# Gate projections of two tiles as one block of seven quarter products, in a one-core Mamba-2 layer

## The chip, the cores and the metric

The kernel runs on one core of a Trainium2 chip. The metric is the device time of one execution in microseconds (us); lower is better. The engines of the core work side by side, each in the order of its own queue: TensorE (PE, matmuls; PEld is its weight load), VectorE (DVE), ScalarE (ACT), GpSimd (POOL) and SyncE (SP), which here issues most of the DMAs.

## What is computed

Two blocks follow each other on x of shape (2, 512, 512), all in fp32. The first is an autocorrelation block with a small mixture of experts. The second, which the change is about, is a Mamba-2 mixer times a gated feed-forward. Cut to that part (B = 2 batches, S = 512 positions, model width 512, inner width 8192 = 128 heads of 64, 8 groups of 16 heads, state 128, chunks of 128):

```python
h = x * rsqrt(mean(x * x) + EPS) * norm_w
proj = einsum("bsd,od->bso", h, in_proj_w)
gate, hBC, dt = split(proj)                 # 8192 | 8192 + 2*8*128 | 128
hBC = silu(causal_conv(hBC, conv_w, conv_b))    # hid, B and C
dt = softplus(dt + dt_bias)
A_full = -exp(A_log) * dt
y = chunked_scan(hid * dt, A_full, B, C) + Dp * hid
yg = y * silu(gate)
ygr = yg * rsqrt(mean over the group of yg * yg + EPS)
out = einsum("bsd,od->bso", ygr * gnorm_w, out_proj_w)
return residual + out
```

The gate is thus a matrix product of 8192 x 512 weights with the 512 x 512 normed input of each batch.

## The kernel before, in words

**Stages.** The first 560 us or so compute the first block, the feed-forward, the normed input hT (features on partitions, L459), the decays, and the tables that go through DRAM. From then on the mixer runs. Its work is cut into units: unit u is group g = u // 2 in batch b = u % 2, 16 of them; each unit has 8 tiles of 128 channels (two heads), so 128 tiles in all.

**Steps.** `step(d)` (L1137) handles two tiles at each of four stages, and there are 64 steps with tiles in the main stage. The tiles `a` are in the main stage; their place in the unit is t = 0, 2, 4 or 6. `p` are the two tiles before them, `n` the two after, `h` the two after those. In a step:
- `products(a)` (L859) multiply decayed scores and start states into y, into a PSUM bank of tag "yy"; `finish_y` (L887) scales and adds D times hid on VectorE.
- `channels(h)` (L993) project the hidden channels into a bank of tag "pj"; `conv` (L839) is one ScalarE and three VectorE operations on that bank; silu follows later (L1227).
- `decays(n)` (L936) turn broadcast sums "cs" into decays: four ScalarE operations and an exponential per head, then a product with CB on VectorE. `starts(n)` (L974) is GpSimd's product of C with the broadcast "eb".
- `transposed` and `values` (L914, L920) turn hid and scale it; `states(n)` (L953) multiply it with B and run the recurrence.
- `gate(a)` (L983) projects each tile's gate: four matmuls of 128x128 weights by 512 columns into "pj" (`project`, L833), and `gate_silu` evicts it with silu into "sgt". In the next step GpSimd multiplies y by it (L1170), ScalarE squares (L898), GpSimd sums the squares.
- At t = 0, `inner` (L1001) projects B and C of the next unit, into "pj" too; `inner_products` (L1010) make the transposed B and the scores CB at t = 2.
- `Output` (L1031) is the output projection of the previous unit. It is already done in Strassen's way: seven products of quarters, each of four matmuls by 256 columns; `sums` (L1058) on GpSimd make the sums of y's quarters, `multiply` (L1071) the products in banks "of" and "yy", `add` (L1111) accumulates them on VectorE. The sums of the weights' quarters (`sum_out`, L785, four GpSimd operations of 128x1024) follow on the scaling of the weights by gnorm_w (`scale_out`, L773, eight VectorE operations). Both are done once per group: in the step t = 0 of odd units from 3 on (for unit 0's group in unit 0's step t = 2). These steps are called made steps here, after the flag `made` (L1212).

[...]

**Order.** The mixer is under a manual schedule (L477): every engine runs its instructions in the order of the text of `step`, and only waits for data and for buffers. PSUM has eight banks, by tags: yy 2, pj 2, tr 2, de 1, of 1. A buffer of a tag with n buffers is handed out in turn, and its new user waits for all readers of the old. SyncE's queue in a step: eb of n, cs of h, gate weights, hidden weights, and at its end el (`load_rest`, L818).

Of the kernel before, what the change touches and what calls it, by code (L numbers as in the profile page):

```python
# [8 lines left out]
F32 = mybir.dt.float32  # L9
I32 = mybir.dt.int32  # L10
AF = mybir.ActivationFunctionType
# [37 lines left out]
def fused_kernel(  # L49
# [407 lines left out]

    mix = ctx.enter_context(tc.tile_pool(name="mix", bufs=1, side="left"))
    hT = mix.tile([P, KD, T], F32, tag="hT", name="hT")  # L459
    Dcol = mix.tile([P, DIN // P], F32, tag="Dcol", name="Dcol")  # L460
    cw = mix.tile([P, (DIN + 2 * NG * NST) // P, KCONV], F32, tag="cw", name="cw")
    cb = mix.tile([P, (DIN + 2 * NG * NST) // P], F32, tag="cb", name="cb")
# [15 lines left out]
    with ExitStack() as l1:  # L478
# [33 lines left out]
        def prepare():  # L512
# [27 lines left out]
            for b in range(B):  # L540
# [6 lines left out]
                def row(tag, name, shape=(P, NCH, NH)):  # L547
                    return tmp.tile(list(shape), F32, tag=tag, name=f"{name}{b}")
# [28 lines left out]
                for r, rt in enumerate(rts):  # L577
# [8 lines left out]
                nc.vector.tensor_tensor(  # L586
                    z, ps, dtb.unsqueeze(1).to_broadcast([P, NCH, NH]), ALU.add
                )
                u, v, q2 = row("u", "u"), row("v", "v"), row("q2", "q2")
                nc.scalar.activation(u, z, AF.Abs)  # L590
                nc.scalar.activation(u, u, AF.Exp, scale=-1.0)
# [144 lines left out]
    with ExitStack() as sm:  # L736
# [12 lines left out]
        def place(s):  # L749

            u, t = divmod(s, GT)
            g, b = divmod(u, B)
            return u, g, b, t, 2 * t
# [52 lines left out]
        def load_sums(s):  # L806

            u, g, b, t, h0 = place(s)
            m = wk.tile([P, 2, S], F32, tag="cs", name=f"cs{s}", bufs=4)
            nc.sync.dma_start(  # L810
                m.rearrange("p h i -> p (h i)"),
                cs_d[b, g * GH + h0 : g * GH + h0 + 2, :]
                .rearrange("h i -> (h i)")
                .partition_broadcast(P),
            )
            css[s] = m
# [12 lines left out]
        def load_slice(g):  # L829
            sls[g] = wk.tile([P, 4, NT, GH], F32, tag="sl", name=f"sl{g}")  # L830
            nc.sync.dma_start(sls[g], sl_d[g])

        def project(w_of, b, ps):  # L833
            for k in range(KD):
                nc.tensor.matmul(  # L835
                    ps, w_of(k), hT[:, k, bass.ts(b, S)], start=(k == 0), stop=(k == KD - 1)
                )
# [45 lines left out]
        def y_of(s):  # L883
            u, t = divmod(s, GT)
            return yqs[u, t // 4][:, t % 4, :]
# [94 lines left out]
                ALU.mult,  # L980
            )

        def gate(s):  # L983
            u, g, b, t, h0 = place(s)
            pg = psum.tile([P, S], F32, tag="pj", name=f"gt{s}", bufs=2)
            project(lambda k: wgs[s // 2][:, k, bass.ts(s % 2, P)], b, pg)
            return pg

        def gate_silu(s, pg):
            sgs[s] = wk.tile([P, S], F32, tag="sgt", name=f"sgt{s}")  # L990
            nc.scalar.activation(sgs[s], pg, AF.Silu)  # L991

        def channels(s):  # L993

            u, g, b, t, h0 = place(s)
            hid[s] = wk.tile([P, S], F32, tag="hid", name=f"hid{s}", bufs=4)
            ps = psum.tile([P, S], F32, tag="pj", name=f"pjh{s}", bufs=2)
            project(lambda k: whs[s // 2][:, k, bass.ts(s % 2, P)], b, ps)
            return ps, g * GT + t, hid[s]

        def inner(u, j):  # L1001

            g, b = divmod(u, B)
            kept, name = ((BTs, "BT"), (CTs, "CT"))[j]
            kept[u] = wk.tile([P, S], F32, tag=name, name=f"{name}{u}", bufs=j + 1)
            ps = psum.tile([P, S], F32, tag="pj", name=f"pjbc{u}_{j}", bufs=2)
            project(lambda k: wbc[g][:, k, j, :], b, ps)
            return ps, DIN // P + j * NG + g, kept[u]

        def inner_products(u):  # L1010

            pb = psum.tile([P, NCH, P], F32, tag="tr", name=f"pb{u}", bufs=2)
            for c in range(NCH):
                nc.tensor.transpose(pb[:, c, :], BTs[u][:, bass.ts(c, P)], ident)
            pc = psum.tile([P, NCH, P], F32, tag="yy", name=f"pc{u}", bufs=2)
            for c in range(NCH):
                nc.tensor.matmul(
                    pc[:, c, :],
                    BTs[u][:, bass.ts(c, P)],
                    CTs[u][:, bass.ts(c, P)],  # L1020
                    start=True,
                    stop=True,
                )
            Bss[u] = wk.tile([P, NCH, NST], F32, tag="Bs", name=f"Bs{u}")
            nc.scalar.copy(Bss[u], pb)
            CBs[u] = wk.tile([P, NCH, P], F32, tag="CB", name=f"CB{u}")
            nc.vector.tensor_tensor(
                CBs[u], pc, upper.unsqueeze(1).to_broadcast([P, NCH, P]), ALU.mult
            )
# [107 lines left out]
        def step(d):  # L1137
# [3 lines left out]
            h = [s for s in (2 * d + 4, 2 * d + 5) if 0 <= s < tiles]  # L1141
            u, g, b, t, _ = place(2 * d)
            went = 0 <= u - 1 < units
            o = outs.get(u - 1)


            projected = 0 if d == -2 else u + 1 if t == 0 and 0 <= u < units - 1 else None
            multiplied = 0 if d == -1 else u + 1 if t == 2 and 0 <= u < units - 1 else None

            pys = [products(s) for s in a]  # L1150


            if h and h[0] % (B * GT) == 0:
                load_slice(h[0] // (B * GT))
            for s in n:
                load_starts(s)
            for s in h:
                load_sums(s)
            if b == 1 and t == 0 and 0 < g < NG:
                load_out(g)  # L1160
            if n:
# [6 lines left out]

            for s in p:
                nc.gpsimd.tensor_tensor(y_of(s), y_of(s), sgs.pop(s), ALU.mult)  # L1170
            if t == 2 and went:
                o.sums(0)
            if d == -1:
# [10 lines left out]
            for s in n[:1]:  # L1184
                decays(s, 1)
                starts(s)
            first = [channels(s) for s in h[:1]]
            for s in n[1:]:
                decays(s, 0)
            for x in first:  # L1190
                conv(*x)
            for s in n[1:]:
                decays(s, 1)
                starts(s)
            for f in [square(s) for s in p]:
                f()

            pxs = [transposed(s) for s in n]
            hcd = [values(s, px) for s, px in zip(n[:1], pxs)]
            if o and t > 0:  # L1200
                o.multiply(2)
            if projected is not None:
                conv(*inner(projected, 0))
            hcd += [values(s, px) for s, px in zip(n[1:], pxs[1:])]
            second = [channels(s) for s in h[1:]]
            if o and t > 0:
                o.add()
                if t == 4:
                    o.sums(1)
            for x in second:  # L1210
                conv(*x)
            made = (g == 0 and b == 0 and t == 2) or (0 < g < NG and b == 1 and t == 0)  # L1212
            if made:
                scale_out(g, 0)
            if projected is not None:
                conv(*inner(projected, 1))
            if made:
                scale_out(g, 1)
                sum_out(g, 0)
                sum_out(g, 1)  # L1220
            if multiplied is not None and d >= 0:
                inner_products(multiplied)
            pg = [gate(s) for s in a[:1]]
            if o and t > 0:
                o.multiply(1)
            for dst in silus:
                nc.scalar.activation(dst, dst, AF.Silu)  # L1227
            silus.clear()
            for s, x in zip(a, pg):
                gate_silu(s, x)  # L1230
            if o and t > 0:
                o.add()
            for s, x in zip(n, hcd):
                states(s, x)
            if t == 0 and went:
                pss = psum.tile([P, NCH], F32, tag="of", name=f"ssq{u - 1}")
                for c in range(NCH):
                    nc.tensor.matmul(
                        pss[:, c : c + 1],
                        sums[u - 1][:, bass.ts(c, P)],  # L1240
                        ones[:, 0:1],
                        start=True,
                        stop=True,
                    )
            if o and t > 0:
                o.multiply(1)
            pg = [gate(s) for s in a[1:]]
            if o and t > 0:
                o.add()
                if t < 6:  # L1250
                    o.multiply(1)
            for s, x in zip(a[1:], pg):
                gate_silu(s, x)
            if t == 0 and went:
                rgs[u - 1] = wk.tile([P, NCH], F32, tag="rg", name=f"rg{u - 1}")
                rsqrt(rgs[u - 1], pss, 1.0 / GW)
            if o and t > 0:
                o.add()
            if t == 6 and 0 <= u < units:
                outs[u] = Output(u)  # L1260

# [22 lines left out]
            nc.vector.tensor_tensor(last, last, q, ALU.add)  # L1284
        o.sums(0)
        o.todo = [(p, i) for i in range(7) for p in range(2)]
        extra = [wk.tile([P, 2, S], F32, tag="cs", name=f"s_last{i}", bufs=4) for i in range(2)]
        extra = [x.rearrange("p h (t i) -> p h t i", t=4) for x in extra]
        o.room = lambda p: [extra[0][:, 0], extra[0][:, 1], extra[1][:, 0]]
        o.banks = lambda p: (("of", 1), ("yy", 2)) if p == 0 else (("pj", 2), ("yy", 2))  # L1290
# [94 lines left out]
```

## Time and profile before

| What | Value |
|---|---|
| Time, median of 3 runs | 2370.71 us (2370.69 to 2370.76) |
| Profiled execution: time / span | 2371.27 us / 2369.6 us |
| TensorE busy | 2313.2 us |
| VectorE / ScalarE / GpSimd busy | 1328.3 / 1165.2 / 888.1 us |
| Steps t = 0, 2, 4, 6 of a unit, from first channels to first channels | 27.2, 29.3, 28.0, 26.3 us |
| Steps t = 2, 4 and 6 of unit 0, from the same rows | 22.0, 20.3, 19.4 us |
| Granted TensorE clock, 600 to 2330 us | 1.00 of full |

How to read it: the span runs from the first to the last instruction on the core. A group's row has the line, the engine, the operation, output<-inputs by the program's names, the shapes and the count; then the busy time in total and the mean of one in ns; then the time that the engine was idle just before instructions of this group, and what ended it. In a timeline a row is one instruction or several alike in a row: start, duration until the last one's end, engine, line and operation. The matmuls' durations are from issue to modelled end and overlap their neighbours. A row of stretches gives for each stretch its length, then busy time with the number of instructions for PE, PEld, DVE, ACT and POOL, the granted clock, the DMA share and GB/s.

### The profile page before, as it was taken

Reading aid. Unit: us, or ns where it says so; the run is one execution under the profiler, and the core shown is the slowest. Engines: PE = TensorE matmul, PEld = TensorE weight load, DVE = VectorE, ACT = ScalarE, POOL = GpSimd, SP = SyncE. Lnnn points to the kernel's source line nnn. Section 1 sums busy time; section 2 is a strip of 40 time slices with the busy share of each in tenths; the row PEclk is TensorE's granted clock in tenths of the full one; section 3 lists DMA queues with packets and bytes.
Section 4 is the critical chain, followed back from the end, with each engine's and each line's share of the span. In section 5 each row is a group of like instructions: output and inputs, shape, how many; then the busy total and the mean of one; then the engine's idle time right before and its main releaser. Section 6 shows DMA issues by size and latency. Waiting matters only on the chain.

```text
span 2369.6 us, 30117 instructions
## 1 busy us (share of the span) xinstructions
PE 2313.2 (98%) x10816; PEld 1410.4 (60%) x10816; DVE 1328.3 (56%) x2500; ACT 1165.2 (49%) x2377; POOL 888.1 (37%) x640
## 2 busy tenths in 40 slices
PE   7989999999999999999999999999999999999997
PEld 4545445544556666666666666666666666666665
DVE  5263434523775556665656566565666565656563
ACT  3141122203675656565556565655656565556550
POOL 4151200001254344433533453436345433533465
PEclk9999999999999999999999999999999999999999
DMA  4021331133454345443534454454445443534452
GB/s 162 0 72 53 98 101 49 53 129 115 126 173 121 117 131 176 132 140 116 155 116 131 137 171 131 125 152 120 124 132 184 129 126 116 156 120 124 140 155 89
DMA packets 187684, 290.13 MB, mean 122 GB/s; under 512 B 15632, under 2 KB 127376, under 8 KB 187152
## 3 DMA queue, kind: packets, MB, share of 16 engines
q1 hardware_dynamic: 186256, 284.02, 39.6%
q0 software_dynamic: 1280, 4.20, 0.5%
q8 instruction: 86, 1.41, 0.2%
q14 instruction: 62, 0.51, 0.1%
HBM read 278.19 MB, written 9.96 MB: 122 GB/s over the span
## 4 chain that ended last, share of the span: by engine, by line
PE 92%; DVE 2%; POOL 2%; issue 2%; ACT 1%; DMA 0%; SPq 0%; POOLq 0%; ACTq 0%; DVEq 0%
PE gt L835 18%; PE pjh L835 18%; PE of L1101 13%; PE py L865 5%; PE pjbc L835 5%; PE pf L708 4%; PE pu L678 4%; PE pg L678 4%; PE pn L958 4%; PE py L874 3%; PE sh L415 2%; PE px L917 2%; PE ofy L1101 2%; PE hu L304 2%; PE ro L389 1%
## 5 line engine op out<-in xcount | busy, mean ns | idle before, releaser
L835 PE MATMUL pjh<-hT,wh 128*128 128x512 f32 x1024 | 467.0, 599 | 0.8 <-issue 0.8
L835 PE MATMUL gt<-hT,wg 128*128 128x512 f32 x1024 | 461.8, 594 | 0.5 <-ACT sq L906 0.5
L1170 POOL TENSOR_TENSOR y<-y,sgt 128x512 f32<-128x512 f32 x126 | 163.0, 1296 | 572.4 <-ACT sgt L991 572.4
L976 POOL TENSOR_TENSOR eb<-CT,eb 128x768 f32<-128x768 f32 x128 | 236.3, 1854 | 309.2 <-DMA eb<-ea_d 266.6
L846 DVE SCALAR_TENSOR_TENSOR hid<-pjh,cw,hid 128x511 f32<-128x511 f32 (+2 forms) x384 | 287.3, 748 | 80.7 <-ACT hid L841 70.6
L942 ACT ACTIVATE cs<-cs,sl 128x128 f32<-128x128 f32 x1024 | 323.5, 388 | 0.0
L835 PEld LDWEIGHTS gt<-hT,wg 128*128 128x128 f32 x1024 | 191.7, 190 | 209.8 <-issue 205.5
L835 PEld LDWEIGHTS pjh<-hT,wh 128*128 128x128 f32 x1024 | 189.1, 190 | 205.9 <-issue 200.3
L1115 DVE SCALAR_TENSOR_TENSOR acc<-of,rg,acc 128x256 f32<-128x256 f32 x192 | 91.0, 481 | 271.2 <-PE of L1101 270.6
L991 ACT ACTIVATE sgt<-gt 128x512 f32<-128x512 f32 x128 | 75.5, 590 | 312.2 <-PE gt L835 312.2
L951 DVE TENSOR_TENSOR cs<-de,CB 128x512 f32<-128x512 f32 x256 | 175.5, 686 | 85.3 <-ACT de L950 82.1
L841 ACT ACTIVATE hid<-pjh,cb,cw 128x512 f32<-128x512 f32 x128 | 98.9, 772 | 200.2 <-PE pjh L835 200.2
L865 PE MATMUL py<-cs,hc 128*64 128x128 f32 x2048 | 180.7, 276 | 0.0
L950 ACT ACTIVATE de<-cs 128x512 f32<-128x512 f32 x256 | 154.1, 602 | 37.4 <-DVE cs L951 32.9
L893 DVE TENSOR_TENSOR y<-py,el 128x512 f32<-128x512 f32 x128 | 87.8, 686 | 115.4 <-PE py L874 115.0
L874 PE MATMUL py<-eb,st 128*64 128x128 f32 x1536 | 149.5, 273 | 0.6 <-issue 0.6
L910 POOL TENSOR_TENSOR sums<-sums,sq 128x512 f32<-128x512 f32 x110 | 139.8, 1271 | 20.7 <-DVE cs L951 11.9
L865 PEld LDWEIGHTS py<-cs,hc 128*64 128x64 f32 x2048 | 121.8, 137 | 35.2 <-issue 34.4
L964 DVE SCALAR_TENSOR_TENSOR st<-st,sl,pn 128x64 f32<-128x64 f32 x512 | 103.8, 276 | 41.2 <-ACT st L960 41.2
L1101 PE MATMUL of<-wt,y 128*128 128x256 f32 x512 | 120.8, 380 | 0.6 <-DVE acc L1115 0.6
L1101 PE MATMUL of<-wo,s 128*128 128x256 f32 x496 | 117.4, 380 | 0.0
L835 PE MATMUL pjbc<-hT,wbc 128*128 128x512 f32 x256 | 116.2, 597 | 0.0
(250 smaller groups left out, 3464.6 us busy)
## 6 DMA issues: line engine op xcount, KB each, us to landing
cs<-cs_d SPq DMA_DIRECT2D x128, 512.0 KB, 6.6
eb<-ea_d SPq DMA_DIRECT2D x256, 192.0 KB, 3.9
wg<-in_in_wT SPq DMA_DIRECT2D x65, 512.0 KB, 8.6
wh<-in_in_wT SPq DMA_DIRECT2D x64, 512.0 KB, 10.5
el<-ea_d SPq DMA_DIRECT2D x256, 128.0 KB, 8.2
wo<-in_out_wT SPq DMA_DIRECT2D x16, 1024.0 KB, 10.1
wbc<-in_in_wT SPq DMA_DIRECT2D x16, 256.0 KB, 9.3
q_g<-in_gate_qT SPq DMA_DIRECT2D x3, 1024.0 KB, 5.2
```

The source lines that it names most:

```text
L678: nc.tensor.matmul(ps[kind], w[kind][:, k, bass.ts(i, P)], xn1T[b][:, k, :], start=(k == 0), stop=(k == KD - 1),)
L835: nc.tensor.matmul(ps, w_of(k), hT[:, k, bass.ts(b, S)], start=(k == 0), stop=(k == KD - 1))
L846: nc.vector.scalar_tensor_tensor(dst[:, j:], ps[:, : S - j], cw[:, ct, KCONV - 1 - j : KCONV - j], dst[:, j:], ALU.mult, ALU.add,)
L865: nc.tensor.matmul(py[bass.ts(hh, HP), bass.ts(c, P)], hc[:, c, bass.ts(hh, HP)], M[:, hh, bass.ts(c, P)], start=True, stop=(c == 0),)
L874: nc.tensor.matmul(py[bass.ts(hh, HP), bass.ts(c, P)], st[:, c - 1, bass.ts(hh, HP)], cte[:, hh, bass.ts(c - 1, P)], start=False, stop=True,)
L910: nc.gpsimd.tensor_tensor(sums[u], sums[u], q, ALU.add)
L942: nc.scalar.activation(m[:, bass.ts(c, P)], m[:, bass.ts(c, P)], AF.Relu, bias=sls[g][:, 3, b * NCH + c, h0 + hh : h0 + hh + 1], scale=-1.0,)
L950: nc.scalar.activation(pe, m, AF.Exp, scale=-1.0)
L951: nc.vector.tensor_tensor(m, pe, CBs[s // GT].rearrange("p c i -> p (c i)"), ALU.mult)
L976: nc.gpsimd.tensor_tensor(eb_t[s], CTs[s // GT][:, P:].unsqueeze(1).to_broadcast([P, 2, S - P]), eb_t[s], ALU.mult,)
L1101: nc.tensor.matmul(ps, x[:, k, :], y[:, k, :], start=(first and k == 0), stop=(k == 3), skip_group_check=True,)
L1170: nc.gpsimd.tensor_tensor(y_of(s), y_of(s), sgs.pop(s), ALU.mult)
```

## The change

The gates of the step's two tiles are projected as one product of a 256 x 512 by a 512 x 512 matrix, both cut into quarters, by seven products of 128x256 by 256x256 quarters or their sums (Winograd's form of Strassen's scheme) instead of eight.
- Four differences of hT's quarters are made once per batch on GpSimd during preparation (`th`).
- Four sums of the gate weights' quarters are made per step on GpSimd (`sw`, one buffer), ahead of the output's sums.
- The products P1 to P7 are accumulated in one "pj" bank for both halves and one "yy" bank for P2. Intermediate sums are copied out by ScalarE (three copies), added to by VectorE (three adds) and passed through silu by three ScalarE operations at the step's end.
- B and C are projected into the bank "of"; the sums of squares go to "yy"; the inner products are made at the end of t = 4; Bs and CB have one buffer each, cs three; cs is loaded one tile later and ahead of eb in SyncE's queue.
- The order of the step is written anew.

The diff, cut (the loading of cs and the ends are as described):

```diff
+    th = mix.tile([P, B, 4, 2, HD], F32, tag="th", name="th")
...
+                for dst, p, q_ in ((t1, b12, b11), (t2, b22, t1), (t3, b22, b12), (t4, b21, t2)):
+                    nc.gpsimd.tensor_tensor(dst, p, q_, ALU.subtract)
...
-        def gate(s):
...
+        class Gates:
+            def __init__(self, s):
...
+                sw = wk.tile([P, 4, 2, P], F32, tag="sw", name=f"sw{s}", bufs=1)
+                s1, s2, s3, s4 = (sw[:, i] for i in range(4))
+                for dst, x, y, op in (
+                    (s1, a21, a22, ALU.add),
+                    (s2, s1, a11, ALU.subtract),
+                    (s3, a11, a21, ALU.subtract),
+                    (s4, a12, s2, ALU.subtract),
+                ):
+                    nc.gpsimd.tensor_tensor(dst, x, y, op)
...
+                self.factors = {
+                    1: (a11, b11),
+                    2: (a12, b21),
+                    3: (s4, b22),
+                    4: (a22, t4),
+                    5: (s1, t1),
+                    6: (s2, t2),
+                    7: (s3, t3),
+                }
+            def multiply(self, *which):
...
+                    ps = self.py if i == 2 else self.ps[:, int(i in (3, 5))]
+                    x, y = self.factors[i]
+                    for k in range(2):
+                        nc.tensor.matmul(
...
+            def copy(self, i, j):
...
+                nc.scalar.copy(self.quarter(i, j), self.ps[:, 0])
+            def add(self, i, j):
...
+            def silu(self):
+                nc.scalar.activation(self.quarter(1, 0), self.ps[:, 0], AF.Silu)
+                nc.scalar.activation(self.quarter(1, 1), self.quarter(1, 1), AF.Silu)
+                nc.scalar.activation(sgs[self.s], sgs[self.s], AF.Silu)
...
-            ps = psum.tile([P, S], F32, tag="pj", name=f"pjbc{u}_{j}", bufs=2)
+            ps = psum.tile([P, S], F32, tag="of", name=f"pjbc{u}_{j}")
```

The new order of a step after `products(a)` and the loads, as the text of the new `step` has it (o is the previous unit's output, absent at t = 0 and in unit 0; "B" and "C" only at t = 0):

```python
for s in p: y *= gate                  # GpSimd
gates = Gates(a[0])                    # GpSimd, four sums
if t == 2: o.sums(0)                   # GpSimd
finish_y(a0); decays(n0, 0); finish_y(a1); decays(n0, 1); starts(n0)
channels(h0); transposed(n0), transposed(n1); o.multiply(1); B
conv(h0); decays(n1, 0); decays(n1, 1); starts(n1); values(n0)
gates.multiply(1, 5); channels(h1); gates.copy(0, 0); gates.multiply(2, 6)
conv(B); values(n1); o.add(); o.multiply(1); gates.add(0, 0)
square(p); conv(h1)
if made: scale_out(g, 0)
gates.copy(0, 1); o.add(); silu of hid and B; states(n)
gates.multiply(7); gates.copy(1, 1); gates.add(1, 1); o.multiply(1); C
gates.multiply(4, 3); o.add(); gates.add(0, 1); conv(C)
if made: scale_out(g, 1); sum_out(g, 0); sum_out(g, 1)
o.multiply(2 if t < 6 else 1)
if t == 0: sums of squares             # TensorE
gates.silu(); silu of C
if t == 0: rsqrt                       # VectorE, ScalarE, VectorE
o.add()
if t == 4: inner_products
```

## The prediction, made before the change was run

> **What bounds the kernel now.** I read the page first: busy shares, the chain that ended last, the costliest groups.
>
> ```profile
> PE 2313.2 (98%) x10816; PEld 1410.4 (60%) x10816; DVE 1328.3 (56%) x2500; ACT 1165.2 (49%) x2377; POOL 888.1 (37%) x640
> ...
> PE 92%; DVE 2%; POOL 2%; issue 2%; ACT 1%; DMA 0%; SPq 0%; POOLq 0%; ACTq 0%; DVEq 0%
> ...
> L835 PE MATMUL gt<-hT,wg 128*128 128x512 f32 x1024 | 461.8, 594 | 0.5 <-ACT sq L906 0.5
> ...
> L1170 POOL TENSOR_TENSOR y<-y,sgt 128x512 f32<-128x512 f32 x126 | 163.0, 1296 | 572.4 <-ACT sgt L991 572.4
> ```
>
> TensorE is the bound, and the gates are a fifth of its work. Next the busy time in stretches:
>
> ```profile
> 800.00:1000.00 200.00, 200.00 (x1066) 128.39 (x1063) 124.13 (x238) 120.34 (x252) 89.80 (x61) 1.00 0.46 137
> 1000.00:1200.00 200.00, 200.00 (x1042) 128.53 (x1041) 124.98 (x240) 118.95 (x248) 89.17 (x59) 1.00 0.49 144
> ```
>
> Between 800 and 2200 PE (second number) never idles. So matmul time removed there is gained in full, and equally every new wait of PE is lost in full: the question is what the reordered step makes PE wait for. For durations I use distances between starts in TensorE's timeline, because the 594 ns above are overlapping lives:
>
> ```profile
> 1319.64 1.89 PE L1101 MATMUL ofy<-wo,y 128*128 128x256 f32 x8
> 1321.37 3.60 PE L835 MATMUL gt<-hT,wg 128*128 128x512 f32 x8
> 1324.80 1.89 PE L1101 MATMUL of<-wt,s 128*128 128x256 f32 x8
> ```
>
> A gate tile (8 instructions of 512 columns) takes 1324.80 - 1321.37 = 3.43 us, 429 ns each; 8 of 256 columns take 1.73 us, 216 ns each. Last, GpSimd's timeline where the output weights' sums are made, ahead of a t=2 step whose products begin at 1380.1:
>
> ```profile
> 1376.17 2.35 POOL L790 TENSOR_TENSOR wt<-wo 128x1024 f32<-128x1024 f32 x1 [10.10 <-DVE wo L777]
> 1378.59 2.35 POOL L791 TENSOR_TENSOR wo<-wo 128x1024 f32<-128x1024 f32 x1
> 1381.02 2.36 POOL L793 TENSOR_TENSOR wt<-wo 128x1024 f32<-128x1024 f32 x1
> 1383.46 2.71 POOL L794 TENSOR_TENSOR wt<-wo,wt 128x1024 f32<-128x1024 f32 x1
> 1386.14 2.96 POOL L1170 TENSOR_TENSOR y<-y,sgt 128x512 f32<-128x512 f32 x2
> ```
>
> GpSimd is busy with them for 1386.14 - 1376.17 = 9.97 us, then 2.92 us with y times gate, 9 us into the next step. Nobody on PE needs either soon. That is what the change alters.
>
> **The matmuls.** Per step two tiles cost 2 x 3.43 = 6.86 us. Seven products of 4 instructions of 256 columns cost 28 x 0.216 = 6.05. Saved 0.805 us, by 64 steps: **-51.5 us**. [...] The row is this very shape with weights changing at each matmul, at a ratio of 0.504; its 190 ns weight loads fit under 216. I take the row.
>
> **The step as PE wants to run it** (us from the step's start; products 3.2, channels 3.54 with the switch, transposes 0.87, an output product 1.73, a gate product 0.865, states 1.34). With output work: first channels end at 6.74, transposes 7.61, output 9.34, P1 and P5 11.07, second channels 14.5, P2 and P6 16.25, output 18.0, states 19.3, P7 20.2, output 21.9, P4 and P3 23.65, two outputs 27.1. Each new wait against it:
> - *Second channels need the first's bank* (one pj bank is now held by the gates). Their conv ends, as in the trace, 6.78 us after the first channels began: 3.2 + 6.78 = 9.98, wanted at 11.07. No wait, if ACT and DVE are free at 6.9; the decays ahead end by 5.9 in the trace. GpSimd's earlier sums can stretch L894 (752 ns median, 1959 at most); 0.7 us of DVE idle takes that.
> - *P6 waits for the copy* of P1. ACT has first to do the decays of the second tile, until about 11.2; copy (nearest rows 128x128 0.265, 128x512 0.58; I take 0.4) 11.6. Wanted at 15.4. The sums cs of that tile are now loaded in this very step: issued at 1.8 behind the first products, 6.6 us to landing, 8.4 against 7.6 when ACT turns to them; 0.8 us of a slack of 3.8.
> - *P4 waits for copy and add of P7's bank.* ACT silus end 19.2, state copies 19.8, copy 20.75; DVE state updates 21.1, add 21.5 (128x512 from PSUM takes 0.69, so 0.42). [...] Zero by either, by 0.4 us; bound 0 to 0.5 us in about 50 steps.
> - *The pool of gates' weights.* Four sums of 128x256 (L291 is this shape, median 0.73 us) are 2.9 us a step of GpSimd, behind y times gate (2.6). In ordinary steps silu ends about 2 us before the step, so the first sum is there at about 1.5; P5 wants it at 10.2. Nothing.
> - ACT gets 2.5 us for 1.2, DVE 1.3 more, per step of some 27: covered, as both stay near 60%. SP issues cs (0.42 each) ahead of the four eb (0.58 each); these land perhaps 4 us later, GpSimd's products with them run at about 10 instead of 6 and 8, and are read a step later. The weight DMAs go 1 us later, also for the next step. The hT differences (8 of 1.27 us) fall where the page shows GpSimd idle. B and C through "of" have a step's room; inner products at the end of t=4 instead of in t=2 cost the same 1.3 us and their products are wanted 4 us later.
>
> **Where it waits: made steps.** At t=0 of odd units (3 to 15) the output weights are scaled and summed. Before, scaling ended 1376.08 - 1352.9 = 23.2 us into the step. Now its second half stands behind C's conv, which stands on DVE behind the gates' last add. In that step P3 ends at 25.4 (channels, B, C: 4 x 3.45 among it), add 26.0, conv 28.2, scaling (1.66) 29.9. GpSimd: four sums 9.97 to 39.9, y times gate 2.92 to 42.8, then s1 to 43.6. The step is 27.23 - 0.8 = 26.4 long, P5 is 10.2 into the next: 36.6. PE waits **7.0 us** (bounds 5.5 to 9, by one us of either chain). Queued behind P5 on PE is everything. Nothing absorbs it, PE being full. The trace has a small forerunner: the one wait of gt for ACT's square in the first fence (0.5 us) falls in unit 0's t=4, behind the same four sums. Six times: **+42.0**.
> - Unit 15 has no B and C, so P4 waits for the add: state updates end at 20.2 behind scaling, add 20.7, wanted at 16.9: 3.8; then 5.0 for s1. **+8.8**.
> - Unit 0 has no output products to fill in. t=2 (scales too): 4.2; t=4: 7.5 for s1 and 3.1 at P4; t=6: 3.9. Less the 1.6 that the kernel idles there now: **+17.1** (8 to 22).
> - After t=0 of even units (2 to 14) C's silu comes after conv (28.2), then table and root to 30.5 (loads 1.28): decays begin 4.1 into t=2, first conv ends at 12.1 where second channels want 11.07: 1.1, seven times: **+7.7** (0 to 14). In odd units the longer wait covers it.
> - End: the last silu is half a us later: +0.6.
>
> **Sum:** -51.5 + 42.0 + 8.8 + 17.1 + 7.7 + 0.6 = +24.7. The profiled execution took 2371.27 (span 2369.6 and 1.7 around it), 0.56 over the median; on the median 2370.71 this gives **2395**.
>
> **Rivals.**
> - *The sums come in time* (not slower). If the first sum reaches P5 in made steps, because DVE scales before the last add or GpSimd's order differs from the text, 42.0, 5.0 and 7.5 go: 2341; with the bank waits of unit 0 gone too, 2320. The page has GpSimd at 37%, which speaks for it; against it, that its five operations in the fence run in the text's order, and that DVE waits in order as well. It decides from a delay of scaling under 23 us into the step.
> - *The shared bank of the channels waits in every step.* If conv ends 1 us later than I have it, PE loses up to 0.9 us in 50 steps: 2440. For it: the slack is only 1.1; against: both engines idle just before.
> [...]
>
> **How the numbers follow.** Forecast 0.70, within it 2366 to 2425: its low end has 5.5 us per made step, half of unit 0 and no wait in even units; the high end 9 us and some of P4's bound. Sums in time 0.16, shared bank 0.12, short matmuls 0.02. 0.2% is 4.7 us, about what a measurement tells from no change. Faster: 0.16 and 0.04 of the forecast's low end, 0.20; same 0.08; slower 0.72. The range 2350 to 2430 leaves out most of the first rival, and a part of the second.
>
> **What would show it.** In the waits, PE's gt standing on the new POOL sums about 50 us in 7 or 8 waits of some 7 us, all in t=2 steps of odd units and one in unit 0; gate starts 0.865 us apart per product; elsewhere PE full. I am wrong if those waits are absent, if PE waits at pjh in each step for DVE's conv, or if 256-column gates are farther apart than 216 ns.

## The result, and the profile after

The changed kernel takes 2427.52 us (median of 4 runs, 2420.83 to 2427.89) against 2370.74 us of the kernel before: 1.0232 times as long, 95% interval 1.0215 to 1.025. That is 56.8 us slower, where the prediction had 24.7: the right way, at less than half the size. The profiled execution took 2427.49 us with a span of 2425.8.

From the page of the changed kernel, the span, the busy times, the chain that ended last by engine, and the gate products with sums:

```profile
span 2425.8 us, 32550 instructions
...
PE 2295.0 (95%) x11584; PEld 1576.5 (65%) x11584; DVE 1417.9 (58%) x2692; ACT 1231.3 (51%) x2633; POOL 1088.9 (45%) x904
...
PE 84%; DVE 7%; POOL 5%; ACT 2%; issue 2%; DMA 1%; POOLq 0%; SPq 0%; ACTq 0%; DVEq 0%
...
L1042 PE MATMUL gt<-th,sw 128*128 128x256 f32 x768 | 203.8, 389 | 35.2 <-POOL sw L1018 34.0
```

TensorE fell from 92% to 84% of the chain, VectorE and GpSimd rose to 12% together: TensorE waits for them. But its busy time fell by only 2313.2 - 2295.0 = 18.2 us, although 51.5 us of matmul cycles are gone. So part of what remains runs longer. Whom TensorE waited for in the changed kernel (total, times, longest):

```profile
PE gt L1042 <- POOL sw L1018: 34.0, 8, 7.0
PE py L880 <- DVE rg L106: 14.3, 14, 1.9
...
PE gt L1042 <- DVE sgt L1063: 12.1, 4, 3.2
PE pjh L850 <- DVE hid L861: 11.8, 10, 2.1
```

Three of these the prediction named: the gates' first sum (eight times), the add ahead of P4 and the first channels' conv. The second row it did not have: the second tile's products wait for their "yy" bank, which the sums of squares hold until the root's first operation on VectorE (L106) has read them. TensorE's timeline in a made step (unit 7, t = 2), and GpSimd's beside it:

```profile
1419.42 1.03 PE L1042 MATMUL gt<-hT,wg 128*128 128x256 f32 x4
1425.17 2.08 PE L1042 MATMUL gt<-th,sw 128*128 128x256 f32 x4 [4.72 <-POOL sw L1018]
1427.04 4.26 PE L850 MATMUL pjh<-hT,wh 128*128 128x512 f32 x8
```

```profile
1419.64 2.36 POOL L809 TENSOR_TENSOR wt<-wo,wt 128x1024 f32<-128x1024 f32 x1
1421.95 2.49 POOL L1250 TENSOR_TENSOR y<-y,sgt 128x512 f32<-128x512 f32 x2
1424.39 0.73 POOL L1018 TENSOR_TENSOR sw<-wg 128x256 f32<-128x256 f32 x1
```

P5 waits 4.72 us for the sum that ends at 1425.1, behind the output weights' sums and y times gate. What the prediction did not have is in the second column, the duration: P5 then lasts 2.08 us where P1, as many matmuls of the same shape, lasts 1.03, and the channels take 4.26 us instead of 3.60. The same stretch of the changed kernel in microseconds; the figures behind the busy times are the granted clock, the DMA share and GB/s:

```profile
1420.00:1421.00 1.00, 0.45 (x3) 0.05 (x1) 0.76 (x2) 0.95 (x4) 1.00 (x1) 1.00 1.05 370
...
1424.00:1425.00 1.00, 0.00 (x0) 0.00 (x0) 0.69 (x2) 0.00 (x0) 1.00 (x2) 0.97 1.03 242
1425.00:1426.00 1.00, 0.82 (x2) 0.74 (x3) 0.00 (x0) 0.00 (x0) 0.92 (x3) 0.50 0.78 172
1426.00:1427.00 1.00, 1.00 (x3) 0.78 (x3) 0.00 (x0) 0.00 (x0) 1.00 (x2) 0.50 0.24 74
1427.00:1428.00 1.00, 1.00 (x3) 0.44 (x2) 0.00 (x0) 0.66 (x2) 1.00 (x2) 0.50 0.00 0
1428.00:1429.00 1.00, 1.00 (x4) 0.43 (x3) 0.00 (x0) 0.76 (x2) 0.92 (x2) 0.82 0.00 0
1429.00:1430.00 1.00, 1.00 (x4) 0.52 (x3) 0.00 (x0) 0.00 (x0) 1.00 (x2) 1.00 0.00 0
```

The granted clock is 0.50 from the wait's end on, for some 3.4 us. Added up over the mixer from such rows of 1 us (one minus PE's busy time is idle; busy time by one minus the clock is what the slow clock costs):

| From the first step with products (598) to the last (2367) | Predicted | Measured |
|---|---|---|
| Matmuls saved, 64 steps (t = 6 steps: 26.26 to 25.44 us) | -51.5 | -52 |
| TensorE idle, less what it idles in the kernel before | +75.6 | 77.9 - 3.1 = +74.8 |
| Slow clock, less 0.7 before | 0 | 26.9 - 0.7 = +26.2 |
| Rest: restarts that the records don't show as waits, and the ends | +0.6 | +7 |
| Sum | +24.7 | +56.2 of span |

The 75.6 are the prediction's 42.0 (made steps), 8.8 (unit 15), 17.1 (unit 0) and 7.7 (other t = 2 steps); recorded as idle are 36.6, 7.8, 18.3 and 12.1. The waits thus came out as forecast in kind, and that their sum fits so well is in part luck, since errors of both signs cancel. The clock had no term.

Lengths of steps from first product to first product, in us, are used below. Without waits a t = 2 step would take 29.32 - 1.33 (inner products, now in t = 4) - 0.8 = 27.2.

| Step | Before | Changed |
|---|---|---|
| t = 0, 4, 6 of units 2 to 14 | 27.23, 27.99, 26.26 | 26.39, 28.49, 25.44 |
| t = 2, made (units 3 to 13) | 29.32 | 35.7 to 37.3, mean 36.3 |
| t = 2, others | 29.32 | 29.14 |
| Unit 0, four steps | 88.8 | 110.3 |

### The profile page after: what moved, and what is told of

It reads as the page before. It is cut to its first block, busy times and chain, and to the rows that moved or that the text cites. A ratio compares the mean times of both kernels' runs of the same rounds, so it can differ in the third digit from the quotient of the medians.

```text
span 2425.8 us, 32550 instructions
## 1 busy us (share of the span) xinstructions
PE 2295.0 (95%) x11584; PEld 1576.5 (65%) x11584; DVE 1417.9 (58%) x2692; ACT 1231.3 (51%) x2633; POOL 1088.9 (45%) x904
## 4 chain that ended last, share of the span: by engine, by line
PE 84%; DVE 7%; POOL 5%; ACT 2%; issue 2%; DMA 1%; POOLq 0%; SPq 0%; ACTq 0%; DVEq 0%
PE pjh L850 18%; PE gt L1042 13%; PE of L1180 12%; PE pjbc L850 4%; PE py L880 4%; PE pf L723 4%; PE pu L693 4%; PE pg L693 4%; PE pn L973 3%; PE py L889 3%; PE sh L415 2%; PE gty L1042 2%; PE ofy L1180 2%; PE hu L304 2%; PE px L932 2%
## 5 line engine op out<-in xcount | busy, mean ns | idle before, releaser
L850 PE MATMUL pjh<-hT,wh 128*128 128x512 f32 x1024 | 479.2, 612 | 13.7 <-DVE hid L861 11.8
L991 POOL TENSOR_TENSOR eb<-CT,eb 128x768 f32<-128x768 f32 x128 | 230.1, 1817 | 297.5 <-DMA eb<-ea_d 280.7
L1250 POOL TENSOR_TENSOR y<-y,sgt 128x512 f32<-128x512 f32 x126 | 157.7, 1273 | 423.1 <-ACT sgt L1070 423.1
L850 PEld LDWEIGHTS pjh<-hT,wh 128*128 128x128 f32 x1024 | 194.1, 195 | 223.9 <-issue 203.5
L861 DVE SCALAR_TENSOR_TENSOR hid<-pjh,cw,hid 128x511 f32<-128x511 f32 (+2 forms) x384 | 286.9, 747 | 88.8 <-ACT hid L856 79.8
L1042 PE MATMUL gt<-th,sw 128*128 128x256 f32 x768 | 203.8, 389 | 35.2 <-POOL sw L1018 34.0
L1042 PEld LDWEIGHTS gt<-th,sw 128*128 128x128 f32 x768 | 143.4, 195 | 55.4 <-POOL sw L1018 37.2
L1059 ACT COPY sgt<-gt 128x256 f32<-128x256 f32 x192 | 71.6, 373 | 160.8 <-PE gt L1042 153.3
L979 DVE SCALAR_TENSOR_TENSOR st<-st,sl,pn 128x64 f32<-128x64 f32 x512 | 103.8, 275 | 51.5 <-ACT st L975 51.2
L909 DVE SCALAR_TENSOR_TENSOR y<-hid,Dcol,y 128x512 f32<-128x512 f32 x128 | 130.3, 1018 | 4.5
L1068 ACT ACTIVATE sgt<-gt 128x256 f32<-128x256 f32 x64 | 24.5, 383 | 203.4 <-DVE sgt L1063 203.4
```

The costliest lines, as they stand in the source:

```text
L850: nc.tensor.matmul(ps, w_of(k), hT[:, k, bass.ts(b, S)], start=(k == 0), stop=(k == KD - 1))
L861: nc.vector.scalar_tensor_tensor(dst[:, j:], ps[:, : S - j], cw[:, ct, KCONV - 1 - j : KCONV - j], dst[:, j:], ALU.mult, ALU.add,)
L991: nc.gpsimd.tensor_tensor(eb_t[s], CTs[s // GT][:, P:].unsqueeze(1).to_broadcast([P, 2, S - P]), eb_t[s], ALU.mult,)
L1042: nc.tensor.matmul(ps, x[:, k, :], y[:, k, :], start=(i in (1, 2) and k == 0), stop=(k == 1), skip_group_check=True,)
```

## The experiments

My theory: the matmul saving is worth its full length; it is lost in waits in made steps (the gates' sum behind the output weights' sums) and smaller ones, and each longer wait is followed by half a clock. Rivals: the short matmuls themselves cost more, or another engine became the bound; the slow clock comes from something else than idleness.

**The matmuls alone.** eight_short and seven_short start from the kernel before:

```diff
-            project(lambda k: wgs[s // 2][:, k, bass.ts(s % 2, P)], b, pg)
+            for k in range(KD):        # seven_short: range(KD - 1 if s % 2 else KD)
+                for j in range(2):
+                    nc.tensor.matmul(
+                        pg[:, bass.ts(j, HD)],
+                        wgs[s // 2][:, k, bass.ts(s % 2, P)],
+                        hT[:, k, b * S + j * HD : b * S + j * HD + HD],
...
```

> The kernel before, with each 128x512 gate matmul cut into two of 256 columns and nothing else: eight products, no sums. Theory (a matmul's price is proportional to its columns, weight loads hidden): 2371 to 2374. [...]

> As eight_short, but the second tile of each step leaves out its last quarter of the contraction (its gates are sums over 384 of 512 features), so that the gates take 28 instead of 32 short instructions a step, without sums, copies or a new order. Theory (the matmul saving is worth its full length where nothing new waits): 51.5 us less than eight_short, about 2320 (2317 to 2324). Rival (something else, ScalarE or GpSimd, takes over as the bound once TensorE has less to do): 2335 or more.

Measured: eight_short 2373.24 us (ratio 1.0008, interval 1.0 to 1.0016), seven_short 2319.61 us (0.9784, 0.977 to 0.9797). Cutting the columns costs 2.0 us (interval 0 to 3.8). seven_short leaves out an eighth of the gates' work, and that is worth 2373.2 - 2319.6 = 53.6 us, or 51.6 against the kernel before. In stretches of seven_short TensorE stays full and ahead of the others:

```profile
800.00:1000.00 200.00, 200.00 (x1149) 148.69 (x1148) 128.53 (x245) 121.43 (x251) 94.25 (x64) 1.00 0.50 148
```

So the step of the matmuls stands, with the row's 216 ns (an instruction; each matmul of the program is two of them, the gates' 512 being 1024 on the page of before). The loss lies in the sums, the evictions and the order.

**The sums' place in GpSimd's queue.** sums_late moves the output weights' sums behind the gates' sums of the next step, sw_first the gates' sums ahead of y times gate:

```diff
# sums_late
                 scale_out(g, 1)
-                sum_out(g, 0)
-                sum_out(g, 1)
+                unsummed.append(g)
...
             gates = Gates(a[0]) if a else None
+            for w in unsummed:
+                sum_out(w, 0)
+                sum_out(w, 1)
+            unsummed.clear()
# sw_first
+            gates = Gates(a[0]) if a else None
             for s in p:
                 nc.gpsimd.tensor_tensor(y_of(s), y_of(s), sgs.pop(s), ALU.mult)
-            gates = Gates(a[0]) if a else None
```

> The changed kernel with the four sums of the output weights issued on GpSimd after the next step's gate sums instead of ahead of them; nothing else. Theory (PE waits in made steps for the gates' first sum, and the slow TensorE clock comes only with those waits): the made t=2 steps of units 3 to 13 fall from 36.3 us to the 29.1 of the other t=2 steps (6 x 7.1 = 43), unit 15's from 31.3 to 29.1, unit 0's t=4 from 34.1 to about 24; some 55 us in all, about 2372 (2366 to 2380). Rival 1 (the late sums only hand the wait on, to the output's own sums): the wait moves to the output products and the time stays above 2400. Rival 2 (the slow clock comes from the denser stream of short matmuls, not from waits): the steps still show a granted clock under 1 and the time stays 20 us or more above 2372.

> The changed kernel with the four gate sums put ahead of the two products of y and gate on GpSimd. Theory: the first sum is there 2.5 us sooner in made steps, so the wait at the second gate product falls from 4.7 to about 2.2 us; the half clock may still come. 8 x 2.5 = 20 us less, 2407 (2398 to 2415). Rival (the wait is for something else on GpSimd, the output weights' sums themselves): no change.

Measured: sums_late 2402.59 us (1.0126, 1.0108 to 1.0145), sw_first 2396.71 us (1.0105, 1.0089 to 1.012). Both are faster than the changed kernel, by 25 and 31 us, and both wait less for sums; but sums_late missed its 2372. The wait for sums in sw_first, then TensorE's longest waits in sums_late:

```profile
PE gt L1042 <- POOL sw L1018: 15.4, 8, 4.6
```

```profile
PE py L880 <- DVE rg L106: 27.5, 14, 4.1
PE pjh L850 <- DVE hid L861: 13.9, 12, 2.1
PE gt L1042 <- DVE sgt L1063: 12.2, 4, 3.2
```

In sums_late no wait for the gates' sums is left: the output weights' sums ahead of them were the cause of those eight. But the wait of the second tile's products for their bank has grown, to 4.1 us in made steps, and these still last 33.1 to 34.4 us. The bank is freed by the root's first operation (L106) on VectorE, which stands behind the scaling. The scaling's second half in a made step of the changed kernel, then of sums_late:

```profile
1409.82 1.66 DVE L792 TENSOR_SCALAR wo<-wo,gn 128x512 f32<-128x512 f32 x4
```

```profile
950.42 3.86 DVE L792 TENSOR_SCALAR wo<-wo,gn 128x512 f32<-128x512 f32 x4
```

The same four operations take 3.86 us instead of 1.66 where GpSimd works beside them (from 949.6 on it multiplies y by the gates; in the changed kernel it idled until the scaling was done). These 2.2 us are what the wait has grown by, from 1.93. The rival of sums_late was half right: a wait was handed on, though not to the output's sums but to the products, by way of a slower VectorE. sw_first came out 1.3 us under its range: made steps fell by 3.6 us on average, to 32.7, of which 0.8 is slow clock, and t = 2 steps that are not made fell too, from 29.14 to 28.57. There VectorE's last operation on y ahead of the first channels' conv took 0.77 us instead of 1.35 (unit 2). Which work of GpSimd it meets may decide that; it was not tried.

**Half the clock.** fill changes nothing but that TensorE repeats P1 where it would wait:

```diff
...
-                gates.multiply(1, 5)
+                waits = (
+                    7 if u == 0 and t == 4
+                    else 1 if u == units - 1 and t == 2
+                    else 4 if g > 0 and b == 1 and t == 2
+                    else 0
+                )
+                gates.multiply(1)
+                gates.again(waits)
+                gates.multiply(5)
```

> The changed kernel as it is, with TensorE repeating the gates' first product where it would wait for the first sum (4 times in the made steps, 7 in unit 0, once in unit 15; same result, the wait ends at the same moment). Theory (half the clock after idleness): the time falls by the half clock behind these waits, 6 x 1.5 to 2 us and 2 to 4 us in unit 0: 2411 to 2417. Rival: no change, 2427.

Measured: 2412.60 us (1.0173, 1.016 to 1.0187), 14.9 us less than the changed kernel, though TensorE does more; the slow clock's cost in the mixer falls from 26.9 to 10.0 us. If a wait cost only its own length, filling it could not shorten the kernel. ssq_early_fill does the same on top of ssq_early, which moves the sums of squares and the root's first operation ahead of C, so that all waiting of a made step falls on P5:

```diff
+            if t == 0 and went:
...
+                nc.vector.tensor_scalar(rgs[u - 1], pss, 1.0 / GW, EPS, ALU.mult, ALU.add)
             third = [inner(projected, 1)] if projected is not None else []
...
-                rsqrt(rgs[u - 1], pss, 1.0 / GW)
+                nc.scalar.activation(rgs[u - 1], rgs[u - 1], AF.Sqrt)
+                nc.vector.reciprocal(rgs[u - 1], rgs[u - 1])
```

> The changed kernel with the sums of squares and the first VectorE operation of their root put ahead of C's projection, so that the second tile's products at t=2 no longer wait for their bank. Theory: the wait of 1.9 us at the products in made steps goes, but the gates' first sum comes at the same moment, so the wait there grows from about 4.7 to 6.6 us and the steps stay as long; only the half clock after the products' wait (units 5, 13) goes. In the other t=2 steps 0.3 us. 2415 to 2426. Rival (each wait costs its own length): 14 x 1 to 2 us less, about 2405.

> As ssq_early, and in the made steps TensorE repeats the gates' first product while it would wait for the first sum (7 times of 0.865 us, in unit 15 4 times; the result is the same, the wait ends at the same moment). Theory (idle TensorE is granted half the clock for some 3 us afterwards): no half clock after these waits, 1.5 to 2.5 us less per made step, 12 to 18 us less than ssq_early. Rival (the slow clock has another cause, or is only a matter of the records): the same time as ssq_early within 3 us, or more.

Measured: ssq_early 2448.63 us (1.0325, 1.0308 to 1.0341), ssq_early_fill 2429.26 us (1.0245, 1.0229 to 1.0262): 19.4 us less by filling. The made step of unit 5 in ssq_early, then in ssq_early_fill:

```profile
1205.21 2.08 PE L1042 MATMUL gt<-th,sw 128*128 128x256 f32 x4 [7.63 <-POOL sw L1018]
1207.08 4.62 PE L850 MATMUL pjh<-hT,wh 128*128 128x512 f32 x8
```

```profile
1189.17 6.21 PE L1055 MATMUL gt<-hT,wg 128*128 128x256 f32 x28
1197.00 1.13 PE L1042 MATMUL gt<-th,sw 128*128 128x256 f32 x4 [1.62 <-POOL sw L1018]
1197.97 3.60 PE L850 MATMUL pjh<-hT,wh 128*128 128x512 f32 x8
```

P5 starts at the same place in the step (18.0 us after its first product in both: 1205.2 - 1187.2 and 1197.0 - 1179.0), but with the wait filled it takes 1.13 and the channels 3.60 us. The made steps are 35.1 us in all six units against 36.7 to 37.3. In these steps slow clock after a wait is thus a consequence of TensorE having been idle.

ssq_early itself missed its expectation, upwards. Its other t = 2 steps last 31.6 us, not 29.1: the sums of squares delay C by 0.8 us, C's conv and silu hold up ScalarE's decays, and the two waits of 0.34 and 1.19 us become one of 2.5 with half the clock behind it. In ssq_early_fill six of eight such steps have the same 2.5 us of wait and no slow clock (29.9 us), two have both (31.6). What decides is where the wait falls in time. In each of the twelve traces, all changes of the granted clock lie on one grid of 3.413 us from the first to the last, to within 1 ns. Two such steps of ssq_early_fill in stretches of this grid, unit 1 and then unit 2:

```profile
743.16:746.57 3.41, 1.30 (x3) 0.68 (x4) 2.61 (x5) 2.66 (x8) 3.41 (x4) 1.00 1.10 270
746.57:749.99 3.41, 3.41 (x5) 1.35 (x4) 3.08 (x6) 1.19 (x3) 2.85 (x2) 0.50 0.38 101
```

```profile
852.39:855.80 3.41, 2.21 (x11) 1.60 (x9) 3.34 (x5) 3.35 (x9) 3.41 (x3) 1.00 1.07 364
855.80:859.21 3.41, 2.10 (x5) 1.06 (x6) 2.65 (x5) 2.71 (x8) 3.41 (x3) 1.00 1.15 282
859.21:862.63 3.41, 3.41 (x14) 2.35 (x13) 3.16 (x7) 1.25 (x3) 2.05 (x2) 1.00 0.17 50
```

In unit 1 most of the wait falls into one stretch, which leaves TensorE 1.30 us busy of 3.41 (38%), and the next stretch has half the clock. In unit 2 two stretches share the wait (65 and 62% busy), and the clock stays. So it is in all traces from 560 us on: of the stretches at full clock, each of the 96 with TensorE busy for less than 41% was followed by one at 0.50, and none of the 6125 with more than 51%; between these, 13 of 39 were. The traces of the kernel before and of the changed one have 16 of 16, none of 1027 and 2 of 7 of these.

**Taking the waits out of the order.** Three kernels have sums_late's change, the root in the middle of the t = 0 step (between P7's copy and its add, in best2 behind the states), and differ in the rest:

```diff
# best: C's conv ahead of the gates' last add
             for x in third:
                 conv(*x)
+            if gates:
+                gates.add(0, 1)
...
# best2 and best3: second half of the scaling ahead of C's conv; silu of C left to the next step
             if made:
                 scale_out(g, 1)
                 unsummed.append(g)
+            for x in third:
+                conv(*x)
...
-            for dst in silus:
-                nc.scalar.activation(dst, dst, AF.Silu)
-            silus.clear()
+            if d < 0:
...
# best2: P7, its copy and add ahead of the silus and states; best3: only under this condition
+            if gates and not o and projected is None:
+                gates.multiply(7)
+                gates.copy(1, 1)
+                gates.add(1, 1)
```

> The changed kernel with the output weights' sums after the next step's gate sums, the sums of squares and the root in the middle of the t=0 step, and C's conv ahead of the gates' last add. Theory: all t=2 steps come to about 27.2 to 27.6 us, as all their waits (first sum, bank of the products, conv of the first channels) are gone: against sums_late another 14 x 1.5 to 1.9 = 21 to 27 us, about 2348 (2340 to 2356), 1% under the kernel before. Rival (the t=2 steps wait for something not seen yet, such as ScalarE's two more table loads at t=0): about 2372.

> The changed kernel with all waits that were found taken out of the order: output weights' sums after the gate sums, the root in the middle of the t=0 step, silu of C left to the next step, the second half of the scaling ahead of C's conv, and the seventh gate product with its copy and add ahead of the silus and the states. Theory: t=2 steps 27.2 to 27.6 us (12 to 20 us less than in the kernel best), steps without output products 1.5 to 2.5 us less each (4 to 10 us): 2335 to 2347. Rival (the added copies and adds themselves, or VectorE's and GpSimd's contention, keep the t=2 steps at 28 or more): about 2355 to 2362.

> The order of the changed kernel with: output weights' sums after the next step's gate sums, root in the middle of the t=0 step, silu of C left to the next step, the second half of the scaling ahead of C's conv; the seventh product with copy and add ahead of the silus only in steps without output products and without C. Theory: t=2 steps 27.2 to 28 us, t=0, 4 and 6 as in the changed kernel, unit 0's steps as short as in best2: 2340 to 2350. Rival (the t=2 steps keep 0.8 us of wait for the first channels' conv): 2352 to 2357.

Measured: best 2361.47 us (0.996, 0.9946 to 0.9973), best2 2367.91 us (0.9984, 0.9978 to 0.9991), best3 2335.04 us (0.9848, 0.9835 to 0.9861). best came out 5 us over its range: C's conv ahead of the add makes the gates' silu, and with it the decays of the next step, late, and the second channels wait 0.8 us in each t = 2 step (28.2 us); in made steps (29.0 us) output products wait another 0.5 us for the output's own sums, which is what rival 1 of sums_late had said; unit 0's waits remain (102.9 us for its four steps). best2 came out 21 us over its own: it brings unit 0 to 93.0 us, but its t = 2 steps stay at 28.3 to 28.6, and others lose:

```profile
PE of L1180 <- DVE acc L1194: 21.9, 31, 3.8
...
PE gt L1042 <- ACT sgt L1059: 11.7, 20, 1.2
```

With P7's add ahead, VectorE's state updates move back and the output's adds stand behind them, so output products wait in each t = 6 step (0.33 us on record, 26.04 us long against 25.44). In t = 0 steps P7 waits 0.55 us for the copy ahead of it (27.08 us against 26.29). best3 keeps the old place of P7 wherever output products or C fill TensorE, and ended 5 us under its range. Its mixer is without waits from unit 1 to 14: t = 2 steps of 27.36 and, made, 27.6 us. In stretches of best3:

```profile
800.00:1000.00 200.00, 199.96 (x1188) 148.57 (x1187) 135.00 (x263) 132.08 (x287) 116.60 (x94) 1.00 0.48 144
1000.00:1200.00 200.00, 199.96 (x1144) 148.47 (x1143) 139.36 (x274) 131.00 (x283) 116.00 (x92) 1.00 0.47 142
```

It takes 92 us less than the changed kernel and 36 us (1.5%) less than the kernel before, of the 51.5 that the matmuls are worth. Most of what is missing lies in units 0 and 15, which are 8.6 and 7.7 us longer than before less 0.8 a step. VectorE, ScalarE and GpSimd do all the added work at 68, 66 and 58% in these stretches, so that work was never the bound; its place was.

## Why the prediction was half right

- **The matmuls, -51.5 us: right.** seven_short gained 53.6 over eight_short by leaving them out alone, and steps without waits are 0.8 us shorter.
- **Made steps, 7.0 us each: the mechanism was right, the price was not.** GpSimd's queue did hold P5's sum back, and sums_late ends these waits. In unit 7 that sum ended 43.6 us after the first product of the t = 0 step (1425.1 - 1381.5), the very figure given. Measured cost is 36.3 - 27.2 = 9.1 us: 6.1 recorded as idle on average (4.7 at the sum and 1.9 at the products' bank in unit 7), 2.5 of slow clock, 0.5 unrecorded (restarts, an estimate). The step that failed is the sentence "PE waits 7.0 us ... Six times: +42.0" and its likes in units 0 and 15: a wait was priced at its own length. The sum had no term for the half clock after a wait and so put it at nothing, without a reason: 18 stretches of 3.41 us at 0.50, 26 us of the 32 missing. The rest, 7 us put at nothing too, is mostly restarts by the estimate at the end.
- **Waits in other t = 2 steps: right in kind, too small.** 1.1 us seven times were given; 1.95 us came eight times (unit 1 is odd but not made, and was left out). 1.53 are recorded: 1.19 at the second channels, near the 1.1 given, and 0.34 at the products' bank, which the prediction did not have; the remaining 0.4 are two restarts, by the same estimate. In made steps that bank's 1.93 us lie within the wait for the sum and add nothing: ssq_early takes them away, and P5 waits 7.63 us instead.
- **Unit 0: +17.1 given, 110.3 - 88.8 + 3.2 = +24.7 measured**, of which 6.2 are slow clock. **Unit 15**: 8.8 given; its t = 0 and t = 2 steps are 6.8 and 4.1 us longer than they would be without waits, 4.6 of it slow clock, and its t = 4 step, which was given nothing, 2.2.
- **Other waits costed at nothing held in the changed kernel**: one wait of ScalarE for cs (0.7 us), none for the copy of P1 in ordinary steps, and t = 4 and t = 6 steps of units 1 to 14 lost nothing to P4's bank. Where P4 did wait, in units 0 and 15, the add ended it and not the copy (the row of sgt L1063 above), as the prediction had counted: 3.8 us in unit 15 and the like in unit 0, a term that no row of before shows. The changed kernel has four waits for the add, of 2.86 to 3.25 us, 12.1 in all. Longer operations of VectorE beside GpSimd's work (L894 at 910 to 1959 ns in before) were left to 0.7 us of VectorE's idle time; there that was enough, in sums_late it was not.
- **The rivals**: that the sums come in time was wrong as it stands, but its forecast of 2320 to 2341 is what best3 reached, where they do and other waits are gone too. The shared bank of the channels did not wait in ordinary steps, with its 1.1 us of slack. That short matmuls cost more, given 0.02, no run shows: cutting the gates' columns cost 2.0 us of 2371 (interval 0 to 3.8).

The trace of the kernel before has the half clock too, on such a grid: TensorE is busy for 0.71 us of the stretch from 592.58 to 595.99 and has 0.50 in the next, up to 599.41; it is busy for 0.02 us from 2336.79 to 2340.21 and has 0.50 up to 2343.62. The prediction counts twelve waits of 3 us or more (six in made steps, two in unit 15, four in unit 0). Half of 3.41 us for each, an estimate from these stretches, is 20 us; the sum would have been about 45 us of the 57 measured.

## What to carry to other kernels

On a full TensorE a new wait cost its length here and, from about 1.7 us on (an estimate from the 51% above), up to another 1.7 us for each stretch of 3.41 us at 0.50 that followed: price both. Where a wait can't be removed, fill it with matmuls that do no harm, or split it, since two waits of 1.2 and 0.3 us apart from each other never halved the clock here, and one of 2.5 did in 10 of 16 steps of ssq_early and ssq_early_fill. When work is put on an engine with a queue, look for the longest stretch that this queue ever holds, not at its share of busy time: best3 does the added work at a higher share and without the waits, by its order alone.

## What the runs showed of the hardware

- **Half clock.** In the twelve traces the granted clock changed only on a grid of 3.413 us. A stretch of it at 0.50 cost 1.5 us on average in the changed kernel (26.9 over 18), and can cost up to half its length, 1.7 us. After a stretch at full clock with TensorE less than 41% busy it always came (96 of 96), after one with more than 51% never (none of 6125). For a lone wait in a full stream this gives an estimate: under 1.7 us (49% of 3.41) never, from 4.0 us on (twice 59% of 3.41) always, between them by where it falls. In the changed kernel, waits of 1.93 us were followed by half the clock in two of six made steps; in sums_late, those of 4.1 us in six of six.
- **VectorE beside GpSimd.** Four scalings took 3.86 us in sums_late instead of 1.66, single ones up to 1.48 instead of 0.48. Of y's second operations in the changed kernel (L909), the 47 that met no work of GpSimd took 0.75 us each; the 66 with GpSimd busy beside them for over 90% took 0.75 to 2.35, median 1.20. So the factor is up to three. y's first operation (L908, from PSUM) took 0.67 to 0.69 us either way. No run here changes GpSimd's company alone, so a cause is not shown.
- **Restarts.** Each recorded wait costs some 0.2 us more than its record, an estimate from the rows: a gate product lasts 1.03 us on record where the next starts 0.865 us after it, so idle time is counted 0.16 us late, and the first row after a wait lasts 0.07 to 0.1 us longer (1.13 against 1.03 for a gate product in ssq_early_fill, 3.67 against 3.60 for channels in fill).
- **Spread.** The four runs of the changed kernel lie 7 us apart. In best2 the executions of 2364.9 to 2365.7 us have a mean granted clock of 0.994 or 0.995, those of 2369.5 to 2370.1 us 0.991 or 0.992. Waits that fall differently on the grid would do that; that they do is not shown.
